# A last projection that takes its PSUM bank when it begins, and a key request half a quad later

## The chip, the cores and the metric

The kernel runs on one core of a Trainium2 chip. The metric is device time in microseconds (us), the median of several executions. TensorE is called PE, VectorE DVE, ScalarE ACT, GpSimd Pool, and SyncE, which issues most DMAs, SP.

## The reference

x is (2, 2048, 512) in fp32. One layer of attention and one linear layer, each with a residual and a layer norm ahead of it:

```
x = x + attention(layernorm(x))      16 heads of 32, 2 groups of keys and values,
                                     rotary tables on q and k, softmax over 2048 keys, then @ wo + bo
x = x + fp8_linear(layernorm(x))     one scale for the whole input, one for the weight,
                                     both rounded to e4m3, product in fp32
```

The one scale of the second part needs the largest magnitude over all tokens, so the second part can begin only when the last token's attention and projection are done.

## The kernel before

**Blocks, quads, units.** The 4096 tokens are eight blocks n of 512 (`TB`), four for each of two batches. The heads are four quads of four. A unit u is half a block (256 queries) of one quad: 64 units, u = 8 n + 2 quad + half. The main loop runs over the units in four rounds r of four key chunks each. Within a round PE makes the shifted scores T (L960), ACT the exponentials p (L969), Pool adds pairs of p (L943) and accumulates them by DMA (L1014, L1016), and PE multiplies p by the values into avs (L910) and sums the pair sums with a matrix of ones (L924). In between, `next(scores)` brings the plain scores of the following unit (PE L517 into s, DVE maximum L524), from which the row maxima come.

**Background work.** Everything else is a generator whose yields name the engine of its next step: `ON_PE`, `ON_DVE` or `OTHER`. A `Job` runs its generator to the first yield when it is made. Jobs stand in three lists, `finishing` (the division of a finished unit, `finish_heads`), `queue` (projections) and `beside` (turning queries, stacking keys, norms). `fill(kind)` takes one step of the first job that is ready and whose next step is of that kind or `OTHER`. The main loop calls `fill(ON_PE)` about seven times in a unit, twice as many in the last two units, and `fill(ON_DVE)` several times.

**The lent bank.** Scores rotate over three PSUM banks s0 to s2. A job that needs PSUM inside the loop calls `bank`, which lends it one of them (`lent[0]`); the scores skip that bank until `give_back`. While a bank is lent, `fill` lets only its owner in `queue` go on, and `do` notes as owner the job whose step made `lent[0]` change. After the loop `attending[0]` is False and the remaining jobs are run to their ends one list after another, in banks of another pool.

**The last block's projection.** For blocks 0 to 6 `finish_block` multiplies the attention by wo (`add_output`, PE L301 into po, DVE L574 adds it to x_res). Block 7 is split: `finish_most` does three of the four chunks of wo for all four token tiles (12 matmuls), and is queued by `finish_heads` of unit 61; `finish_rest` does the fourth chunk for one half (2 matmuls each), queued by `finish_heads` of units 62 and 63. Then come the second norm's statistics, the scale and the fp8 part.

**Keys.** The keys of the attended batch lie stacked in `kS` and `dkS` (two groups, one for quads 0 and 1, one for quads 2 and 3). The next batch's keys are projected during the first batch's blocks, stacked by `stack_keys` and written to DRAM (`halves_far`). `fetch_keys(what, b, g)` issues four DMAs of 256 KB on SP that bring one group into the stack. `stack_next(u)` runs at the start of unit u: on even units it prepares the next quad's queries (calling `advance`, which takes steps of jobs at once, until the query is there) and, in block 3, requests group 0 of batch 1, again calling `advance` until the keys of block 7 are done. Group 1 is requested at the first unit of batch 1.

Of the kernel before, what the change touches and what calls it, by code (L numbers as in the profile page):

```python
# [27 lines left out]
def preln_attn_fp8_ffn_kernel(  # L28
# [38 lines left out]
    B, S, D = x.shape  # L67
    NB = S // TB
# [14 lines left out]
    ON_PE, ON_DVE, OTHER = "PE", "DVE", "other"  # L83
# [268 lines left out]
    def stack(dst, src):  # L352

        for r, part in enumerate(src):
            nc.sync.dma_start(dst(slice(r * HD, (r + 1) * HD)).bitcast(F32), part)

    def fetch_keys(what, b, g):
        far = halves_far[what, b]
        stack(
            lambda rows: stacked[what][rows, g, :],  # L360
            [far[g * HD : (g + 1) * HD, h, :] for h in (0, 0, 1, 1)],
        )
# [76 lines left out]
    keys_done = set()  # L439
# [34 lines left out]
    def stack_queries(k):  # L474

        n, quad = quads[k]
        hi, lo = halves(q_raw.pop((n, quad)), P, f"q_{n}_{quad}")
        qst[k] = wide.tile([P, 4, TB], F32R, tag="qst", name=f"qst_{k}", bufs=2)
        far = dram.tile([P, 2, TB], F32, tag=f"q_far_{k % 2}", name=f"q_far_{k}")
        for h, part in enumerate((hi, lo)):  # L480
            nc.sync.dma_start(far[:, h, :], part.bitcast(F32))
        far = far.rearrange("(j d) h t -> d h j t", j=4)
        read = lambda: stack(
            lambda rows: qst[k][rows, :, :], [far[:, h, :, :] for h in (0, 1, 0, 1)]
        )
        if attending[0]:
            landing.append(read)
        else:
            read()

    def batch(k):
        return quads[k][0] // NB
# [71 lines left out]
    def add_output(n, xt, attn, i, dims=range(DC)):  # L564

        po = bank(f"po_{n}_{i}_{dims[0]}")
        yield from product(
            po,
            lambda c: attn[:, dims[c], i * P : (i + 1) * P],
            lambda c: wo_sb[:, dims[c], :],  # L570
            len(dims),
        )
        yield ON_DVE
        nc.vector.tensor_tensor(xt[:, i, :], po, xt[:, i, :], ALU.add)  # L574
        give_back()

    def second_norm(n, xt, tiles=range(NT)):

        yield from layernorm_stats(
            xt, mean2[:, n, :], rstd2[:, n, :], f"2_{n}_{tiles[0]}", tiles  # L580
        )


        ends = small.tile([P, NT, 2], F32, tag="ends", name=f"ends_{n}_{tiles[0]}")
        for i in tiles:
            for e, op in enumerate((ALU.max, ALU.min)):
                yield ON_DVE
                nc.vector.tensor_reduce(ends[:, i, e : e + 1], xt[:, i, :], AX.X, op)
        at = slice(tiles[0], tiles[-1] + 1)
        yield ON_DVE  # L590
        for e in range(2):
            end = ends[:, at, e]
            nc.gpsimd.tensor_tensor(end, end, mean2[:, n, at], ALU.subtract)
            nc.gpsimd.tensor_tensor(end, end, rstd2[:, n, at], ALU.mult)
        yield LATER
        yield ON_DVE
        nc.vector.tensor_reduce(
            amax2[:, n * NT + tiles[0] : n * NT + tiles[-1] + 1],
            ends[:, at, :],
            AX.X,  # L600
            ALU.max,
            apply_absolute_value=True,
        )
# [15 lines left out]


    def finish_most(n, xt, attn):
        for i in range(NT):
            yield from add_output(n, xt, attn, i, range(DC - 1))

    def finish_rest(n, xt, attn, half):
        tiles = range(half * HT, (half + 1) * HT)
        for i in tiles:
            yield from add_output(n, xt, attn, i, range(DC - 1, DC))
        beside.append(Job(second_norm(n, xt, tiles)))
        y_near[n] = xt  # L630
# [146 lines left out]
    def do(jobs, job):  # L777
        held = lent[0]
        job.step()
        if held is None and lent[0] is not None:  # L780
            owner[0] = job
        if job.kind is None:
            jobs.remove(job)
# [5 lines left out]
    def advance():  # L789
        ready = [job for job in queue if job.due < NEVER and not job.waits()]  # L790
        if lent[0] is not None:
            ready = [owner[0]]
        for jobs, some in ((queue, ready), (beside, list(beside))):
            for job in some[:1]:
                do(jobs, job)
# [21 lines left out]
    def stack_next(u):  # L817
        k, half = units[u]
        n, quad = quads[k]

        if half == 0:
            if k + 1 < len(quads) and k + 1 not in qst:
                while quads[k + 1] not in q_raw:
                    advance()
                stack_queries(k + 1)
            b = batch(k)
            if b + 1 < B and n == (b + 1) * NB - 1:
                if quad == 2:
                    while (b + 2) * NB - 1 not in keys_done:
                        advance()  # L830
                    fetch_keys("kS", b + 1, 0)
                    fetch_keys("dkS", b + 1, 0)
            if b > 0 and n == b * NB and quad == 0:
                fetch_keys("kS", b, 1)
                fetch_keys("dkS", b, 1)

    def ask(u):

# [42 lines left out]
    def finish_heads(u, both, sums):  # L881

        k, half = units[u]
        n, quad = quads[k]
        nc.scalar.copy(both[:, 1, :], sums)  # L885
        for c in range(HB // P):
            yield ON_DVE
            piece = both[:, 1, c * P : (c + 1) * P]
            nc.vector.reciprocal(piece, piece)  # L889
        nc.gpsimd.tensor_tensor(  # L890
            attn_of[n][:, quad, half * HB : (half + 1) * HB], both[:, 0, :], both[:, 1, :], ALU.mult
        )
        if n == NBLK - 1:
            if quad == QUADS - 2 and half == HALVES - 1:
                queue.append(Job(finish_most(n, x_res[n], attn_of[n])))
            elif quad == QUADS - 1:
                queue.append(Job(finish_rest(n, x_res[n], attn_of[n], half)))
        elif quad == QUADS - 1 and half == HALVES - 1:
            job = Job(finish_block(n, attn_of.pop(n)))
            if n not in biased:  # L900
                job.due = NEVER
                without_x[n] = job
            queue.append(job)
# [68 lines left out]
    with tc.manual_schedule():  # L972
        for _ in range(LEAD):
            next(scores)
        for u, (k, half) in enumerate(units):
            n, quad = quads[k]
            if half == 0 and quad == 0:
                attn_of[n] = wide.tile(
                    [P, QUADS, TB], F32, tag="attn", name=f"attn_{n}", bufs=2
                )  # L980
            stack_next(u)
            banks = [
                ps_t.tile([P, 4, HB], F32, tag="EO"[parity], name=f"T_{u}_{parity}")
# [182 lines left out]
```

## Time and profile before

| | us |
|---|---|
| median of 3 runs | 2356.63 (2355.38 to 2365.41) |
| the profiled execution | 2365.06 |
| its span, first to last instruction | 2363.3 |
| PE busy, matmuls | 2145.0 (91%) |
| DVE busy | 1697.7 (72%) |
| Pool busy | 1765.8 (75%) |
| ACT busy | 1231.3 (52%) |
| mean granted TensorE clock | 0.969 |

In the lines of the profile, a group is line, engine, operation, output tile <- input tiles and size, with how often it occurs; in brackets stands how long the engine was idle before it and what released it. "PEld" is PE's weight load, "SPq" a queue's issue of a DMA. In the chain of work that ended last each line is start, duration and what ran. A view of windows has one line per stretch of time: its length, then the busy time and the number of instructions of PE, PEld, DVE, ACT and Pool, the granted clock, the share of DMA engines in use and GB/s.

### The profile page before, as it was taken

To read this page: it belongs to the slowest core of one execution; us is meant where nothing else is said; L and a number is where in the kernel's file an instruction comes from. 1 tells how busy PE (TensorE), PEld (TensorE's weight loads), DVE (VectorE), ACT (ScalarE), POOL (GpSimd) and SP (SyncE) were. 2 spreads that over 40 slices of the span, in tenths; PEclk is the share of its full clock that TensorE was granted. 3 is DMA by queue.
4 is the path that set the end of the run, shared out by engine and by line. 5 is a ranking of instruction groups with operands and counts; after the bars stand their busy time and mean duration, and the time that the engine had idled before them with its cause. 6 is when DMAs were issued, how large, how long until landed. Compare 5 with 4: busy or idle time off the path is not lost. (4 is left out here: it accounts for less than half of the span.)

```text
span 2363.3 us, 39392 instructions
## 1 busy us (share of the span) xinstructions
PE 2145.0 (91%) x15506; PEld 1246.7 (53%) x15506; DVE 1697.7 (72%) x2679; ACT 1231.3 (52%) x1545; POOL 1765.8 (75%) x1199
## 2 busy tenths in 40 slices
PE   5499999999999999999999999999999799899855
PEld 2255555555555555555555555555555455555422
DVE  3467777776687676867767778676876977768378
ACT  2146555655556555645445556454555445555536
POOL 3268889888777987878778878787887777878700
PEclk9689999999999999999999999999999999999977
DMA  6546656666465666657486556564565646847502
GB/s 195 163 102 136 134 117 163 137 138 136 89 167 123 152 134 143 158 116 163 96 204 139 111 118 154 121 120 96 132 146 116 143 91 140 166 85 199 108 32 111
DMA packets 116410, 312.76 MB, mean 132 GB/s; under 512 B 16896, under 2 KB 17536, under 8 KB 112384
## 3 DMA queue, kind: packets, MB, share of 16 engines
q0 software_dynamic: 50160, 175.66, 39.6%
q1 hardware_dynamic: 63648, 133.21, 19.1%
q8 instruction: 121, 1.98, 0.4%
q10 hardware_dynamic: 2416, 1.38, 0.2%
q14 instruction: 65, 0.53, 0.1%
HBM read 91.56 MB, written 42.99 MB: 57 GB/s over the span
## 5 line engine op out<-in xcount | busy, mean ns | idle before, releaser
L524 DVE TENSOR_REDUCE part<-s 128x1 f32<-128x512 f32 x2048 | 1304.8, 683 | 559.6 <-PE s L517 546.0
L943 POOL TENSOR_TENSOR pa<-p,p 128x1024 f32<-128x1024 f32 x511 | 1233.5, 2459 | 300.6 <-ACT p L969 272.7
L969 ACT ACTIVATE p<-T 128x1024 f32<-128x1024 f32 x1024 | 1001.3, 1024 | 590.6 <-PE T L960 564.1
L517 PE MATMUL s<-kS,qst 128*128 128x512 f32 x2048 | 832.4, 465 | 97.0 <-DVE part L524 31.0
L960 PE MATMUL T<-qst,dkS 128*128 128x512 f32 x2048 | 669.7, 423 | 14.4 <-ACT p L969 14.3
L517 PEld LDWEIGHTS s<-kS,qst 128*128 128x128 f32 x2048 | 369.0, 190 | 488.4 <-DVE part L524 256.9
L910 PE MATMUL avs<-p,vX 128*32 128x256 f32 x8192 | 497.7, 383 | 0.8 <-ACT p L969 0.8
L960 PEld LDWEIGHTS T<-qst,dkS 128*128 128x128 f32 x2048 | 365.5, 189 | 161.8 <-ACT p L969 59.4
L910 PEld LDWEIGHTS avs<-p,vX 128*32 128x32 f32 x8192 | 239.7, 110 | 210.4 <-issue 64.7
L1014 POOL DMA_DIRECT2D pa<-pa x255 | 224.3, 880 | 80.4 <-POOL pa L943 75.3
L889 DVE RECIPROCAL both<-both 128x128 f32<-128x128 f32 x128 | 112.4, 919 | 33.8 <-ACT both L885 33.8
L301 PE MATMUL po<-wo_sb,attn 128*128 128x512 f32 x256 | 130.5, 601 | 0.9 <-DVE x_res L574 0.9
L301 PE MATMUL pq<-xnT_q,wq_sb 128*128 128x512 f32 x224 | 113.9, 592 | 0.0
L924 PE MATMUL avs<-pa,ones 128*32 128x256 f32 x1512 | 105.6, 382 | 5.6 <-DMA pa<-pa 5.6
L1032 ACT COPY both<-avs 128x256 f32<-128x256 f32 x64 | 23.8, 373 | 138.3 <-PE avs L910 137.1
L885 ACT COPY both<-avs 128x256 f32<-128x256 f32 x63 | 23.5, 373 | 131.9 <-PE avs L924 131.9
L890 POOL TENSOR_TENSOR attn<-both 128x256 f32<-128x256 f32 x64 | 85.0, 1328 | 6.8 <-DVE both L889 6.8
L951 PEld LDWEIGHTS T<-mT,sel 128*128 128x128 f32 x512 | 80.0, 192 | 12.2 <-issue 0.4
L951 PE MATMUL T<-mT,sel 128*128 128x256 f32 x512 | 82.9, 285 | 0.0
L1016 POOL DMA_DIRECT2D pa<-pa x64 | 74.0, 1156 | 6.5 <-DMA pa<-pa 6.2
L924 PEld LDWEIGHTS avs<-pa,ones 128*32 128x32 f32 x1512 | 49.1, 111 | 39.0 <-DMA pa<-pa 6.5
L503 POOL TENSOR_TENSOR mrow<-mx,mrow 128x8 fp32r<-128x8 f32 x64 | 52.8, 824 | 11.6 <-ACT mrow L532 11.6
(126 smaller groups left out, 1118.7 us busy)
## 6 DMA issues: line engine op xcount, KB each, us to landing
pa<-pa POOLq DMA_DIRECT2D x319, 512.0 KB, 4.7
qst<-q_far SPq DMA_DIRECT2D x128, 256.0 KB, 4.7
x_kv<-in_L_attn_x_dram SPq DMA_DIRECT2D x8, 1024.0 KB, 8.8
q_far<-hi_q SPq DMA_DIRECT2D x32, 256.0 KB, 4.3
q_far<-lo_q SPq DMA_DIRECT2D x32, 256.0 KB, 3.6
x_res<-in_L_attn_x_dram SPq DMA_DIRECT2D x8, 1024.0 KB, 12.3
x_res<-in_L_attn_bo_dram POOLq DMA_DIRECT2D x8, 1024.0 KB, 12.0
out_dram<-v SPq DMA_DIRECT2D x16, 512.0 KB, 2.8
```

Source lines behind the costliest of these rows:

```text
L301: nc.tensor.matmul(dst, lhs(c), rhs(c), start=(c == 0), stop=(c == chunks - 1))
L517: nc.tensor.matmul(s, qst[k][:, j, at : at + P], stacked["kS"][:, group(k), kb * TB : (kb + 1) * TB], start=True, stop=True,)
L524: nc.vector.tensor_reduce(part[:, i, j, kb : kb + 1], s, AX.X, ALU.max)
L889: nc.vector.reciprocal(piece, piece)
L890: nc.gpsimd.tensor_tensor(attn_of[n][:, quad, half * HB : (half + 1) * HB], both[:, 0, :], both[:, 1, :], ALU.mult)
L910: nc.tensor.matmul(av[j * HD : (j + 1) * HD, :], vX[batch(k)][:, kc, group(k), :], p[:, j, :], start=(kc == 0), stop=(kc == NTS - 1), tile ...
L924: nc.tensor.matmul(dst[j * HD : (j + 1) * HD, :], ones, part[:, j, :], start=start and i == 0, stop=stop and i == len(parts) - 1, tile_pos ...
L943: nc.gpsimd.tensor_tensor(pa, a, b, ALU.add)
L951: nc.tensor.matmul(T[:, j, :], sel[:, j, :], maxima[u], start=(j % 2 == 0), stop=True, skip_group_check=True,)
L960: nc.tensor.matmul(T[:, j : j + 2, :], stacked["dkS"][:, group(k), kc * P : (kc + 1) * P], qst[k][:, j : j + 2, half * HB : (half + 1) * H ...
L969: nc.scalar.activation(p, T, AF.Exp, scale=SCALE)
L1014: nc.gpsimd.dma_start(out=far_sums[r], in_=pair, accum_op=ALU.add)
```

## The change

Both generators of block 7's projection begin with `yield OTHER`, as `finish_block` does, so that making the job takes no bank. And the request for group 0 of batch 1's keys, with its `advance` loop, moves from unit 28 (block 3, quad 2, half 0) to unit 29 (half 1). The request for group 1 keeps its place; its condition is written out anew.

```diff
     def finish_most(n, xt, attn):
+        yield OTHER
         for i in range(NT):
             yield from add_output(n, xt, attn, i, range(DC - 1))

     def finish_rest(n, xt, attn, half):
+        yield OTHER
         tiles = range(half * HT, (half + 1) * HT)
...
-            b = batch(k)
-            if b + 1 < B and n == (b + 1) * NB - 1:
-                if quad == 2:
-                    while (b + 2) * NB - 1 not in keys_done:
-                        advance()
-                    fetch_keys("kS", b + 1, 0)
-                    fetch_keys("dkS", b + 1, 0)
-            if b > 0 and n == b * NB and quad == 0:
-                fetch_keys("kS", b, 1)
-                fetch_keys("dkS", b, 1)
+        b = batch(k)
+        if b + 1 < B and n == (b + 1) * NB - 1 and quad == 2 and half == 1:
+            while (b + 2) * NB - 1 not in keys_done:
+                advance()
+            fetch_keys("kS", b + 1, 0)
+            fetch_keys("dkS", b + 1, 0)
+        if b > 0 and n == b * NB and quad == 0 and half == 0:
+            fetch_keys("kS", b, 1)
+            fetch_keys("dkS", b, 1)
```

## The prediction

> **What bounds the kernel now.** The two edits touch two places, so I read those and leave the totals alone. First I cut the span into units, from one copy of a finished unit's sums (ACT L1032) to the next. Unit u is block n = u // 8, quad (u % 8) // 2, half u % 2. The change's first place is units 28 and 29 (block 3, quad 2), the second units 62 and 63 and what follows them. In the view of windows, columns are busy time by engine, granted TensorE clock, DMA share, GB/s. Units 20 to 24 stand first, then 28 to 32.
>
> ```profile
> 773.48:807.75 34.27, 33.63 (x241) 19.44 (x241) 23.25 (x37) 19.02 (x24) 33.01 (x23) 1.00 0.81 190
> 807.75:843.82 36.07, 34.03 (x241) 19.51 (x241) 24.26 (x37) 18.00 (x22) 31.62 (x21) 1.00 0.68 126
> 843.82:877.65 33.83, 33.10 (x239) 19.15 (x239) 24.94 (x38) 17.94 (x23) 29.16 (x20) 1.00 0.61 133
> 877.65:911.87 34.22, 32.80 (x239) 19.22 (x239) 23.35 (x37) 16.85 (x20) 26.82 (x17) 1.00 0.41 78
> 911.87:945.68 33.81, 33.08 (x239) 19.15 (x239) 23.81 (x38) 17.40 (x21) 25.55 (x17) 1.00 0.77 187
> 1038.92:1084.87 45.95, 39.20 (x249) 22.58 (x249) 25.24 (x38) 19.70 (x26) 37.60 (x26) 0.93 0.85 199
> 1084.87:1118.59 33.72, 32.29 (x237) 18.86 (x237) 23.98 (x37) 18.09 (x23) 27.88 (x19) 1.00 0.63 118
> 1118.59:1154.30 35.71, 32.63 (x239) 19.23 (x239) 26.92 (x37) 17.36 (x21) 30.85 (x20) 1.00 0.58 127
> 1154.30:1188.08 33.78, 33.05 (x239) 19.13 (x239) 23.48 (x37) 16.83 (x20) 24.29 (x16) 1.00 0.41 78
> 1188.08:1222.47 34.39, 31.11 (x235) 18.33 (x235) 23.73 (x39) 17.44 (x21) 22.95 (x16) 1.00 0.99 243
> ```
>
> Unit 28 lasts 45.95 us where its neighbours last about 34. The timeline inside it says why.
>
> ```profile
> 1038.73 3.70 PE L301 MATMUL pq<-xnT_q,wq_sb 128*128 128x512 f32 x8
> 1045.92 0.62 ACT L246 CAST hi_kS<-kx 64x512 fp32r<-64x512 f32 x1 [6.11 <-POOL kx L336]
> 1047.18 0.79 PE L517 MATMUL s<-kS,qst 128*128 128x512 f32 x1 [4.52 <-ACT q L450]
> 1076.35 0.70 PE L517 MATMUL s<-kS,qst 128*128 128x512 f32 x2 [1.87 <-DMA qst<-q_far]
> ```
>
> This is the wait loop of `stack_next`: it calls `advance` until the last keys are done, so a whole query projection (8 rows, four instructions) and the key stacking stand in one lump at the head of the unit. ACT waits for Pool's key rotation, the bias copy of the queries stands behind it on ACT, and PE waits 4.52 us for the bank that this copy frees. The clock is at 0.50 from 1047.2 to 1051.2, so a 4-row group takes 1.05 instead of 0.63 us. And qst, queued on SP behind the key loads, holds PE once more at 1076.
>
> The end is read from the chain that ended last (start, duration):
>
> ```profile
> 2233.93 6.59 DMA pa<-pa
> 2240.56 1.93 PE sums_last L924 x16
> 2242.50 14.17 PE po L301 x28
> 2256.69 0.70 DVE x_res L574
> 2257.52 1.97 PE po L301 x4
> 2259.52 0.69 DVE x_res L574
> ```
>
> All 32 projection rows of the last block (one fp32 instruction is two rows) run alone, after the attention. The code says why: `finish_most` takes its bank while the job is being made, inside a `finish_heads` job. `do` then notes that job as the owner of the lent bank, it ends, and `fill` finds no ready job in the queue for the rest of the loop.
>
> **Part 1, keys half a quad later.** The instruction order of the two built programs shows what the scheduler makes of it. In the changed one the lump is gone: the four pq matmuls, the query copy, hi_kS, hi_dkS and Pool's lo_kS, dk, lo_dkS spread over unit 28, and by unit 29 the keys are done, so nothing is forced there. On SP the qst stack, the 1 MB x_res load and sw_q of query 0 now precede the key loads. Units 28 to 32 then carry 7, 7, 2+4, 6 and 6 projection instructions (pq, pq, pq and po, po, po), exactly those of units 20 to 24. So units 20 to 24 price it:
> - before, units 28 to 32: 45.95+33.72+35.71+33.78+34.39 = 183.55;
> - twin, units 20 to 24: 34.27+36.07+33.83+34.22+33.81 = 172.20, that is 11.35 less. The four deferred projections are in it already (unit 32 gets six po for four).
>
> The twin lacks the key loads, eight DMAs of 256 KB each time. Unit 32 has one set, four po and 34.39 us. Unit 25 (no po) lasts 29.25, unit 24 (six) 33.81, so 0.76 per po and 32.29 for four: a set costs up to 2.1 us. Unit 32 keeps its set (+2.1). Unit 29 gets one: 0 at best, as the DMA share there is 0.68; 2.1 at worst by unit 32; I take 1.5, nearer unit 32, because its queue is the same. SP issues them in 3.54+4.00 = 7.5 us (timeline at 1055.5), and in the twin SP has nothing to issue between 805.5 and 814.5, so sw_q of query 1 behind them is hardly late. If that cover were gone, its turn would slip by a round and be taken up at once, since that query is stacked two units on. The keys are read by the next batch's scores from unit 30's last round, some 50 us after the request, against a landing of 6 to 8 us. Sum: -11.35+2.1+1.5 = -7.75. Ends: -11.35 (no load cost) and -5.0 (2.1 in both units and the same again for a late sw_q).
>
> The group-1 request is the same instruction in the same place; it costs nothing.
>
> **Part 2, the bank.** With `yield OTHER` first, `fill` runs the twelve po of `finish_most` inside the loop: 3 in unit 62's last round, 9 in unit 63 (2, 3, 1, 3 by round). Scores are over by then, so the bank is missed by nobody, and `sums_last` takes another one. What is left behind sums_last are four po.
> - Removed at the end: from sums_last's end (2242.43) the last add starts 17.1 us later (2259.52). After: sums copy, two reciprocals and Pool's product end 3.24 after it (2245.67); po_0_3 and po_1_3 (4 rows of 0.43) fit in that; po_2_3 and po_3_3 need the product and take, like the x4 above, 2.03 to the last add. With 0.1 between, 3.24+0.1+2.03 = 5.4. Gain 11.7.
> - Added in units 62 and 63: 24 rows of 0.43 = 10.3 us on PE, and behind each stand the T and avs matmuls that ACT and then Pool wait for. Unit 63 has 23.43-20.11 = 3.3 us of PE idle, unit 62's last round 0.71+0.18+0.43 = 1.3: 5.7 are not covered by gaps. But Pool, not PE, ends the unit: its adds run back to back to 2233, the accumulating DMA lands at 2240.5, and PE's avs were over at 2235.7. Round by round, each po counted at 0.86 less the gap of the timeline that it stands in (0.7 to 0.9 after a round's first T pair, 0.6 before avs), PE falls behind by 1.3 in unit 62's last round, 1.1 in round 0 and 1.25 in round 1; Pool runs 0.5 us behind ACT there, so round 2's adds on Pool, and the DMA after them, come 3.65-0.5 = 3.1 later. I take 3.1; ends 0 and 5.7. A gain is excluded, as nothing on this path is removed.
> - The four adds on DVE (0.69 each): DVE idles 18 us in unit 63, so nothing.
> - `finish_rest` taking its bank later: nothing waits for it before sums_last.
>
> Sum: -11.7+3.1 = -8.6, ends -11.7 and -6.0.
>
> In the window from 2236.0 to 2242.4 PE is mostly idle and gets 0.78, then 0.50 up to 2246.0 and 0.98 after. The Trainium skill ("TensorE: Matmul & The Clock Gate", section "What's actually happening") says that an idle window of about 3.4 us halves the clock and a busy one of that length restores it. This trace agrees (0.50 for 3.6 us). By that rule the fewer PE gaps ahead of sums_last keep the clock full; if it still closed, the estimate would be the second rival's, some 2.6 us later.
>
> **Sum.** 7.75+8.6 = 16.35. The profiled execution took 2365.06 (span 2363.3): it would be 2348.7. It is 8.4 above the median of the runs, 2356.63, and the rows don't say where that lies; both pieces are orders of work that every execution shares, so I subtract the same: 2340.3.
>
> **Rivals.**
> 1. The lump's time comes back. Unit 21, 36.07 us with the heaviest query work, is the one whose twin gets the loads; if they hold up sw_q or Pool's accumulating DMAs there, the 7.75 are lost and 2356.6-8.6 = 2348.0 stays. For: a DMA share of 0.99 in unit 32. Against: that unit is only 2.1 longer. 0.09.
> 2. The clock drops at the end all the same: the last 4 rows at 0.86 instead of 0.43 (+1.7) and half of sums_last's (+0.9): 2342.9. For: Pool and the DMA still end last before sums_last. Against: PE has more to do there. 0.10. This is what the Trainium skill's rule would give if the gap outlived the window.
> 3. PE becomes the bound of unit 63 and all 10.3 us show: tail -11.7+10.3 = -1.4, 2347.5. Against: PE idles 3.3 us there. 0.05.
> 4. Slower: a po that waits for an add or a bank leaves PE idle for some 4 us inside unit 63 and the clock halves there. PE's 20.1+7.7 = 27.8 us would become 55.7 against 23.43: +32.3; with -11.7 and -7.75 that is 2369.4. It decides at a PE gap of 3 to 4 us; the longest now are about 1.1, and the clock is 1.00. 0.04.
>
> That the change doesn't do what it says is excluded by the order of instructions.
>
> **Numbers.** The forecast has 0.72, its own range 2333.6 (both ends on the good side: 23.05) to 2345.6 (5.0+6.0). To hold 8 in 10 the range goes to 2348, over rivals 1 to 3, and to 2332 below, leaving out rival 4 and the scatter of the runs (2355.38 to 2365.41). A measurement tells 0.5% from no change, that is 11.8 us: below 2344.9 lie 0.70 of the forecast's 0.72 and rival 2, so 0.80 faster; 0.02+0.09+0.05 = 0.16 the same; 0.04 slower.
>
> **What would show it.** Right: unit 28 near 34 us with clock 1.00, no PE wait for ACT q at its head; unit 29 at 36 to 38; units 28 to 32 together near 176; the chain's po behind sums_last down from x28 and x4 to eight rows; sums_last ending about 3 us later against unit 62's start. Wrong: unit 29 or 30 above 42 us, a PE wait for kS or qst there, units 62 and 63 together longer by over 6 us, or a clock under 1.00 in unit 63.

## The result and the profile after

The changed kernel took 2344.41 us (median of 4 runs, 2343.33 to 2346.83) against 2359.18 for the kernel before beside it, 14.8 us less: ratio 0.9936, 95% interval 0.9911 to 0.9961. Timed a second time it took 2342.79 against 2363.56: 0.9914 (0.9901 to 0.9928), 20.8 us less. The profiled execution took 2344.18, its span 2342.4, against 2365.06 and 2363.3 before.

The windows of units 28 to 32 after the change, with the columns as before (length; busy time and instructions of PE, PEld, DVE, ACT, Pool; clock, DMA share, GB/s):

```profile
1039.54:1073.85 34.31, 33.67 (x241) 19.44 (x241) 23.24 (x37) 19.03 (x25) 33.05 (x23) 1.00 0.80 190
1073.85:1109.93 36.08, 34.03 (x241) 19.51 (x241) 24.27 (x37) 18.00 (x23) 30.98 (x21) 1.00 0.89 180
1109.93:1143.73 33.80, 33.07 (x239) 19.14 (x239) 25.00 (x38) 17.93 (x22) 29.52 (x20) 1.00 0.64 137
1143.73:1177.97 34.24, 32.78 (x239) 19.22 (x239) 23.35 (x37) 16.86 (x21) 26.85 (x17) 1.00 0.41 77
1177.97:1212.44 34.47, 33.07 (x239) 19.14 (x239) 23.82 (x38) 17.52 (x22) 23.84 (x16) 1.00 0.95 214
```

They last 172.90 instead of 183.55. Against the twin units 20 to 24 the first four differ by 0.04 us at most; the fifth, with the second set of key loads, is 0.66 longer. Unit 28's clock is 1.00 again.

The end, in the chain of work that ended last and in the timeline of PE behind unit 63:

```profile
2225.06 6.56 DMA pa<-pa
2231.66 1.11 PE sums_last L925 x16
2233.27 1.77 DVE both L890 x2
2235.18 0.74 POOL attn L891
2235.96 2.00 PE po L301 x4
2237.98 0.69 DVE x_res L574
```

```profile
2232.66 1.98 PE L301 MATMUL po<-wo_sb,attn 128*128 128x512 f32 x4
2235.96 1.98 PE L301 MATMUL po<-wo_sb,attn 128*128 128x512 f32 x4 [1.31 <-POOL attn L891]
```

Eight po rows are left behind sums_last. The first four run while DVE and Pool make the last quad's product; the other four wait 1.31 us for it. From sums_last's end (2232.77) the last add starts 5.21 later; before it was 17.1. The price stands in units 62 and 63:

```profile
2172.58:2200.89 28.31, 27.62 (x225) 16.52 (x225) 20.61 (x34) 16.76 (x21) 24.22 (x20) 1.00 0.58 126
2200.89:2228.64 27.75, 26.83 (x210) 13.86 (x209) 3.69 (x5) 16.19 (x18) 22.90 (x14) 1.00 0.46 87
```

28.31 and 27.75 for 27.51 and 23.43. I measure the end from unit 61's end to the start of the last add: 74.54 before (2184.98 to 2259.52), 65.40 after (2172.58 to 2237.98), 9.14 less. With 10.65 from units 28 to 32 that is 19.8 of the 20.9 us by which the spans differ. Unit 33 is shorter too, 33.91 for 35.06, so the first place is worth 11.8 in this profile. What is left are units that the change doesn't touch, some longer, some shorter, which cancel here.

### The profile page after: what moved, and what is told of

It reads as the page before. It is cut to its first block, busy times and chain, and to the rows that moved or that the text cites. A ratio compares the mean times of both kernels' runs of the same rounds, so it can differ in the third digit from the quotient of the medians.

```text
span 2342.4 us, 39403 instructions
## 1 busy us (share of the span) xinstructions
PE 2137.7 (91%) x15506; PEld 1243.9 (53%) x15506; DVE 1695.1 (72%) x2679; ACT 1231.1 (53%) x1545; POOL 1765.0 (75%) x1199
## 5 line engine op out<-in xcount | busy, mean ns | idle before, releaser
L952 PEld LDWEIGHTS T<-mT,sel 128*128 128x128 f32 x512 | 79.0, 190 | 12.1 <-issue 0.4
L532 ACT CAST mrow<-mx 128x8 fp32r<-128x8 f32 x64 | 13.1, 205 | 93.4 <-DVE mx L531 93.4
```

Of the source, the lines that this page charges most:

```text
L952: nc.tensor.matmul(T[:, j, :], sel[:, j, :], maxima[u], start=(j % 2 == 0), stop=True, skip_group_check=True,)
```

## The experiments

Units whose code is the same last the same in every kernel to about 0.05 us, apart from a few (8, 32, 40, 41, 48, 52, 53, 58, and 29 by up to 0.5), and unit 0 ends up to 7 us earlier or later. So the medians tell whether, and the units tell where. Unit 33 follows the change: 33.9 us wherever the keys are requested late and nothing is forced in unit 28, 34.5 in e1_bank and e3_lump, 35.06 before; why is not shown.

**e1_bank and e2_keys: each part alone.** e1_bank is the kernel before with

```diff
     def finish_most(n, xt, attn):
+        yield OTHER
...
     def finish_rest(n, xt, attn, half):
+        yield OTHER
```

> Only the two yields; the key request stays in unit 28. If the two parts are independent, this gives the tail alone: units 62 and 63 about 5 us longer together, the stretch from unit 63's end to the last add about 14 us shorter, so 9 us less than the kernel before, unit 28 still at 46. The rival, that the po matmuls cost as much in the loop as they save behind it, gives a change within 2 us.

e2_keys is the changed kernel without these two lines.

> Only the key request half a quad later; the last block's projection as before. Independent parts: units 28 to 32 at 173 instead of 183.5, chain's end with 32 po rows behind sums_last, 8 to 11 us less than the kernel before. The rival, that the lump's time comes back in the following units, gives a change within 2 us.

Measured: e1_bank 0.9972 (0.9961 to 0.9982), 6.9 us less by the medians; e2_keys 0.9951 (0.9936 to 0.9967), 12.3 less. The two together, 19.2, are the change's 20.8 within the intervals: nothing shows that the parts depend on each other. Both rivals (a change within 2 us) fall. e1_bank gained less than the 9 expected, e2_keys more than the 8 to 11; its units 28 to 33 are 12.5 shorter. e1_bank's unit 28 is at 48.62, not at 46: PE waits 3.1 us for qst there instead of 1.9. e1_bank's window of unit 28, then e2_keys' windows of units 28, 29 and 63:

```profile
1033.04:1081.66 48.62, 40.54 (x249) 23.32 (x249) 25.25 (x38) 19.69 (x26) 37.55 (x26) 0.89 0.81 189
```

```profile
1039.80:1074.09 34.29, 33.66 (x241) 19.43 (x241) 23.26 (x37) 19.04 (x24) 33.02 (x23) 1.00 0.83 190
1074.09:1110.16 36.07, 34.02 (x241) 19.51 (x241) 24.27 (x37) 17.98 (x22) 31.68 (x21) 1.00 0.92 181
2199.89:2223.31 23.42, 20.12 (x192) 10.10 (x191) 1.76 (x2) 16.20 (x19) 22.23 (x15) 1.00 0.52 98
```

Each place follows its own part. The end of e1_bank takes 65.46, as in the changed kernel; that of e2_keys 72.52, 2.0 less than the kernel before with the same code there. The difference is in the first po behind sums_last, in e2_keys' chain:

```profile
2229.88 12.24 PE po L301 x28
```

12.24 us for 28 rows is 0.44 a row, at a granted clock of 1.00; before, 14.17 began with 3.6 us at 0.50. So the old end depended on when the clock came back, and the gain at the end is 7 to 9 us.

**e3_lump: the forced steps back in unit 28, the loads at unit 29.**

```diff
+        if b + 1 < B and n == (b + 1) * NB - 1 and quad == 2 and half == 0:
+            while (b + 2) * NB - 1 not in keys_done:
+                advance()
         if b + 1 < B and n == (b + 1) * NB - 1 and quad == 2 and half == 1:
```

> The changed kernel, but unit 28 again forces the jobs on until the last keys are done; the loads stay at unit 29. If the forced lump is the cost, unit 28 is again at 42 to 46 us with a PE wait of some 4 us for ACT q, and the run loses 7 to 10 us of the gain. If the loads queued ahead of qst were the cost, unit 28 is at 34 to 37 and nearly all of the gain stays.

Measured: 0.9961 (0.9947 to 0.9974), 10.1 us less than before: it keeps the gain at the end and little more. Unit 28 lasts 44.19 us, and PE waits at its head as before:

```profile
1042.23 0.50 PE L517 MATMUL s<-kS,qst 128*128 128x512 f32 x1 [4.54 <-ACT q L450]
```

Units 28 to 32 take 180.58, 7.7 more than in the changed kernel. With the loads ahead of qst as well (e1_bank) they take 185.08, 4.5 more again, and PE waits 3.1 us for qst, which e3_lump doesn't. So the lump is the larger part of what was removed, and the loads ahead of qst the smaller (3.0 by the kernel before, 4.5 by e1_bank).

**e4_twice: the eight loads of unit 29 issued twice.**

```diff
             fetch_keys("kS", b + 1, 0)
             fetch_keys("dkS", b + 1, 0)
+            fetch_keys("kS", b + 1, 0)
+            fetch_keys("dkS", b + 1, 0)
```

> The changed kernel with the eight key loads of unit 29 issued twice (the same data again). If a set of loads costs the 2.1 us that the prediction took from unit 32, unit 29 goes from 36.1 to about 38 and the run gets 2 us longer, more if SP's queue of 8 us more delays the turned queries. If the loads are hidden, unit 29 stays at 36.1 and the time within 1 us.

Measured: 0.9951 (0.9935 to 0.9966), 12.1 us less than before where the change gained 20.8. Neither number holds: unit 29 lasts 43.99 us, 7.9 longer. The timelines of DVE and of PE in it say why:

```profile
1106.67 1.85 DVE L319 SCALAR_TENSOR_TENSOR sw_q<-sw_q,sign,cs 128x512 f32<-128x512 f32 x1 [4.65 <-DMA sw_q<-q]
```

```profile
1109.17 1.39 PE L517 MATMUL s<-kS,qst 128*128 128x512 f32 x2 [6.31 <-DVE part L524]
```

SP comes to the swap DMAs of query 1 at 17.5 us into the unit instead of 6.7. The rotation that needs them stands on DVE in front of the score maxima, DVE waits 4.65 us, PE 6.31 for the banks, and the clock is at 0.50 from 1109.2 to 1113.0. This is the first rival's mechanism. One set fits in front of it, two do not.

**e11_more: half a set more** (one more `fetch_keys("kS", b + 1, 0)` in the same place).

> The changed kernel with half a set of key loads more at unit 29 (kS once again, four DMAs, 1 MB). In the changed kernel the rotation of query 1 starts on DVE about 6 us after its swap can have landed, by the 14.7 us from the first swap DMA to the rotation that e4_twice shows. If that slack is what hides the loads, four more DMAs (3.5 to 4 us on SP) still fit and unit 29 stays at 36 to 37. If each load costs in proportion (half of e4_twice's 7.9), unit 29 is at 40.

Measured (one run): unit 29 lasts 37.47, 1.4 longer, between the two expectations. DVE now stands idle for 1.21 us before the rotation:

```profile
1096.89 0.75 DVE L319 SCALAR_TENSOR_TENSOR sw_q<-sw_q,sign,cs 128x512 f32<-128x512 f32 x1 [1.21 <-issue]
```

The swap DMAs start 3.4 us later than in the changed kernel (10.1 into the unit), and the rotation 1.3 us later, so the slack of one set is about 2 us, not the 6 that I read from e4_twice. The profile doesn't name what DVE waited for here; that it is the swap, as in e4_twice, is inferred.

**e9_later: the second set in round 2 of unit 29, behind query 1's swap.**

```diff
+        if n == NB - 1 and quad == 2 and half == 1:
+            fetch_keys("kS", 1, 0)
+            fetch_keys("dkS", 1, 0)
         if half == 0 and quad == 0:
```

> The changed kernel with the second set of key loads of e4_twice, but requested in round 2 of unit 29, behind the swap DMAs of query 1 on SP. If it was the order on SP that made unit 29 last 44.0 us in e4_twice (the swap of query 1 late, DVE waiting for it in order), unit 29 is back at 36 to 38. If the 2 MB of traffic cost it, unit 29 or 30 stays 6 to 8 us longer.

Measured: 0.9915 (0.9901 to 0.9929). Unit 29 is back at 36.92, so it was the order on SP that made it 44 us. The 2 MB are not free all the same: in the profiled execution unit 30 lasts 37.63, 3.8 longer than in the changed kernel. There, by e9_later's timelines of DVE and Pool, the rotation is not late, but long:

```profile
1117.59 4.51 DVE L319 SCALAR_TENSOR_TENSOR sw_q<-sw_q,sign,cs 128x512 f32<-128x512 f32 x1
```

```profile
1116.56 4.99 POOL L947 TENSOR_TENSOR pa<-p,p 128x1024 f32<-128x1024 f32 x2
```

It begins under Pool's two adds and ends 0.55 us after they do. It begins 7.33 us into the unit in both kernels; what moved is Pool, whose adds start 6.30 us into the unit instead of 3.65. Pool's timeline at the end of unit 29 shows what held it up, an issue that waits for an accumulating DMA:

```profile
1105.36 0.85 POOL L1020 DMA_DIRECT2D pa<-pa  x1 [3.63 <-DMA pa<-pa]
```

In the changed kernel Pool doesn't wait there. SP issues the second set from 1090.4 to 1094.5, and the DMA share of that unit is 1.02 instead of 0.89; that this delayed the accumulation is likely, not shown. Two of the five executions took 2340 us, the other three 2346 to 2347 like the profiled one, and the ratio is that of the change: the cost need not come in every execution.

**e5_half and e10_half: half of finish_most in the loop.** The first two token tiles stay in the loop, the others run after it.

```diff
...
-                queue.append(Job(finish_most(n, x_res[n], attn_of[n])))
+                queue.append(Job(finish_most(n, x_res[n], attn_of[n], range(HT))))
+                queue.append(Job(finish_most(n, x_res[n], attn_of[n], range(HT, NT)), due=NEVER))
```

> The changed kernel, but only two of the four token tiles of finish_most go into the loop; the other two (6 po instructions, 12 rows) run after sums_last. If PE is what ends unit 63 and each po there costs most of its 0.86, sums_last ends 1.5 to 3 us earlier, the last add comes 4 to 5 us later after it, and the run is 2 to 3 us longer. If the po were free in the loop, sums_last ends at the same distance and the run is 4 to 5 us longer.

Measured: 0.9931 (0.9919 to 0.9943), 4.4 us longer than the changed kernel. But the edit did another thing too: with half of `finish_most` done early, two po of `finish_rest` came into the loop, and PE met a product that Pool had yet to make:

```profile
2226.21 2.08 PE L301 MATMUL po<-wo_sb,attn 128*128 128x512 f32 x2 [3.98 <-POOL attn L891]
```

Unit 63 lasts 30.81, and those two rows take 2.08 us where two rows elsewhere take 1.02: the granted clock is 0.63 from 2226.2 to 2230.0. It says nothing on the question; it shows the fourth rival in small. e10_half therefore also holds `finish_rest` back (`due=NEVER`).

> Like e5_half, but finish_rest stays behind the loop too, so that PE meets no product of Pool inside unit 63. If PE ends unit 63 and a po costs most of its 0.86 there, the six po that leave the loop bring sums_last 2 to 3 us nearer to unit 61's end (from 60.2 to about 58) and the last add stands about 10 us behind sums_last instead of 5.2: units 62 and 63 and the end together 2 to 3 us longer than in the changed kernel. If po were free in the loop, sums_last stays at 60.2 and the sum is 5 us longer.

Measured (one run), in the windows of units 62 and 63:

```profile
2171.86:2200.18 28.32, 27.62 (x225) 16.50 (x225) 20.61 (x34) 16.77 (x21) 24.24 (x20) 1.00 0.57 126
2200.18:2225.09 24.91, 22.39 (x198) 11.32 (x197) 2.46 (x3) 16.16 (x18) 21.70 (x14) 1.00 0.46 88
```

Unit 63 is 2.84 us shorter for six po fewer, 0.47 each. sums_last ends 58.60 behind unit 61's end instead of 60.19 (1.6 nearer, less than the 2 to 3 expected), the last add starts 9.2 behind sums_last instead of 5.2, and the whole end takes 67.80 instead of 65.40. So a po, 0.86 us on PE, costs about half of that in unit 63's length and 0.27 us at sums_last; behind sums_last it costs 0.67.

**after_again: the change, timed a second time.**

> The changed kernel itself, timed beside the others of this job. From the units of its profile: 20 us less than the kernel before in units 28 to 32 and the end together, of which the medians showed 15. If the parts add up, it stands about 19 us below the kernel before, the sum of what the two parts gave alone (6.9 and 12.3).

Measured: 20.8 us less, given above.

**e8_both: two other lumps taken apart.** On top of the change, block 7's x is loaded later, and the weight's rounding goes to DVE in smaller steps. A third edit, not in the expectation, stands in the same run: in the last unit two of the accumulations by DMA are left out, and sums_last adds their parts by matmul instead.

```diff
-            if n == NBLK - 1:
-                take_x(f"res_{n}")
-                x_res[n] = load_x(n, "res")
-                unbiased.append(n)
+        if n == NBLK - 1 and quad == 2 and half == 0:
+            take_x(f"res_{n}")
+            x_res[n] = load_x(n, "res")
+            unbiased.append(n)
...
             magic = t2(f"w_magic_{o}")
+            yield ON_DVE
             yield from round_e4m3(w[o], v, magic)
...
         nc.vector.tensor_tensor(v, v, magic, ALU.add)
+        yield ON_DVE
         nc.vector.tensor_tensor(dst, v, magic, ALU.subtract)
...
                 if not (last and whole):
                     far_sums.append(add_pair(u, chunks[2], *probs[2:]))
-                    nc.gpsimd.dma_start(out=far_sums[r], in_=pair, accum_op=ALU.add)
-                if r == 2:
+                    if whole and r == 2:
+                        loose = [pair]
+                    else:
+                        nc.gpsimd.dma_start(out=far_sums[r], in_=pair, accum_op=ALU.add)
+                if r == 2 and not whole:
                     nc.gpsimd.dma_start(out=far_sums[1], in_=far_sums[0], accum_op=ALU.add)
...
-        sum_up(sums, [pair, *probs[2:], *far_sums[1:]], True, True)
+        sum_up(sums, [*far_sums, *loose, pair, *probs[2:]], True, True)
```

> The changed kernel with two other lumps taken apart in the same spirit: block 7's x is loaded in unit 60 instead of beside block 6's in unit 56 (unit 58 lasts 40.7 us, with a DMA wait of 4.3 us on PE), and the FFN weight's rounding goes to DVE in single steps (unit 52 lasts 40.4 us, with a PE wait of 5.0 us for DVE). If these waits are the price, units 52, 53 and 58 fall to about 35, 34 and 36 and the run gets some 8 us shorter, less 2 to 4 us for the steps that now stand in units 56 and 57. If the work merely moves, the time stays within 2 us.

Measured: 2329.24 us, 0.9855 (0.9841 to 0.9868) of the kernel before, 13.6 less than the changed kernel timed beside it. Its windows of units 52, 53, 57 and 58:

```profile
1834.41:1867.44 33.03, 29.47 (x234) 17.41 (x234) 32.23 (x46) 18.30 (x22) 29.59 (x20) 1.00 0.76 156
1867.44:1902.74 35.30, 32.76 (x239) 19.23 (x239) 27.46 (x40) 16.91 (x21) 28.07 (x18) 1.00 0.43 82
2001.41:2032.44 31.03, 28.45 (x231) 16.97 (x231) 29.04 (x47) 17.66 (x21) 25.51 (x20) 1.00 0.56 103
2032.44:2066.57 34.13, 32.33 (x239) 19.27 (x239) 26.50 (x43) 17.35 (x22) 27.89 (x18) 1.00 0.65 139
```

They were 40.75, 37.13, 29.77 and 40.43 in after_again's profile. Unit 56, which takes part of the weight's steps, goes from 28.62 to 32.65, unit 57 from 29.77 to 31.03; units 52 to 58 together are 12.6 shorter, more than the 4 to 6 expected, and unit 61 is 1.0 longer. PE's waits of 5.0 us for DVE and of 4.3 us for a DMA, which the changed kernel has in this stretch, are gone. The place of the third edit is 0.8 us shorter: from unit 61's end to the start of the last add it is 64.58 us, for 65.40 in the changed kernel. The three edits were not run apart. This is the fastest kernel of the study.

## Why the prediction was right

The direction, both mechanisms and their places hold, and 2344.4 lies in the range. The step to an absolute time was helped by chance: by the units and by the second timing the gain is nearer to 20 than to the 16.35 predicted (14.8 by the first), while the kernel before ran at 2359 to 2364 here, above the 2356.63 that I subtracted from.

- **The twin units** were the best step: 34.27, 36.07, 33.83, 34.22 predicted units 28 to 31 within 0.04 us each, deferred projections included.
- **The load term was mis-sized.** I put 1.5 us on unit 29 and 2.1 on unit 32; they cost 0.0 and 0.7 in the profile after (0.5 and 0.6 in after_again), and unit 32 lasts 33.79 in e2_keys, no more than its twin. Most of the 3.5 us by which the sum fell short lie here. The 2.1 was a real wait, but not the price of a set. PE's waits in unit 32 (us in total, times, longest), before and then after:

```profile
PE mtp L543 <- POOL mrow L503: 2.1, 1, 2.1
```

```profile
PE mtp L543 <- POOL mrow L503: 0.8, 1, 0.8
```

  In e2_keys this wait is missing, with the same loads requested in the same place. The step for mrow stands on Pool behind an issue that waits for an accumulating DMA, by Pool's timeline before:

```profile
1218.43 0.85 POOL L1016 DMA_DIRECT2D pa<-pa  x1 [3.28 <-DMA pa<-pa]
```

  After the change Pool waits 2.72 us there, in e2_keys 1.83. So PE pays for an accumulation that lands too late for it, and one unit's 2.1 was no price for the next. What made it land earlier is not shown. The slope of 0.76 us per po is not what failed: without these waits (2.1 and 0.6 for qst before, 0.8 after) unit 32 is about 31.7 with four po and 33.7 with six.
- **Unit 33 is not in the sum at all.** It is 1.15 us shorter, in e2_keys as in the changed kernel.
- **The cover was right, what lies behind it wrong.** I wrote that a late sw_q would slip by a round and be taken up at once. e4_twice shows 7.9 us instead: the rotation's place on DVE is fixed when the program is built, so DVE waits in it. The first rival did not happen, but it stands only about 2 us away (e11_more), and its other condition, Pool's accumulating DMAs held up, is what PE felt in unit 32 and Pool in e9_later.
- **The end**: 11.7 predicted behind sums_last, 11.9 measured (17.1 to 5.2). About 2 us of that are luck of the clock: in e2_keys the same old end takes 15.1, which leaves 9.9. 3.1 late at sums_last predicted, 2.7 measured at its end (60.19 for 57.45 from unit 61's end); its last 16 rows begin 3.5 later, and are 0.8 shorter at the full clock. e10_half confirms that PE ends unit 63 in part, which the walk by rounds gave.
- **The second rival** did not come: the clock was 1.00 from 2231.6 to 2236.0, and sums_last's last 16 rows took 1.11 instead of 1.93. The first of PE's two gaps ahead of it had shrunk, by PE's timelines before and then after; the second is 0.79 for 0.78:

```profile
2238.23 0.64 PE L924 MATMUL sums_last<-pa,ones 128*32 128x256 f32 x8 [2.51 <-POOL pa L943]
```

```profile
2229.37 0.64 PE L925 MATMUL sums_last<-pa,ones 128*32 128x256 f32 x8 [0.85 <-POOL pa L944]
```

  The Trainium skill ("TensorE: Matmul & The Clock Gate", section "What's actually happening"), as weighed in the prediction, has the clock halved by an idle window of about 3.4 us. The trace after agrees: no such window, no halved clock. The trace before shows that less was enough: no gap there was longer than 2.51 us, PE was busy for 3.40 of the 6.40 us from 2236.0 to 2242.4, and the clock was at 0.50 behind them. Here the measurement decides.
- **The third** is refuted by e1_bank: not all 10.3 us show, but 2.7 at sums_last. **The fourth** did not happen in the changed kernel; e5_half shows that a gap of 3.98 us in unit 63 is enough for it to begin.

## What to carry to other kernels

Where units of work repeat, find the unit that already does what the change would bring, and price the change with it whole. A wait that one execution shows beside a transfer is not the price of that transfer elsewhere: ask which engine's step was late, and behind what. A forced loop in a builder ("go on until X is done") looks like nothing in the code and was a lump here on PE and ACT at once: look for units that last longer than their neighbours, and ask half a unit later. Before a transfer is put ahead of others on one queue, find whose operands come behind it and how many us they have to spare.

## What the runs showed of the hardware

The same 128x512 rotation on DVE (two operands in SBUF) took 0.65 us where Pool had just finished its adds and 4.51 where it began under them, as shown in e9_later. In the changed kernel's unit 30 it took 1.86, and in after_again's unit 29, the one that is 0.5 us longer, 1.20. In these three it ended 0.55 to 0.57 us after Pool's adds did. The Trainium skill ("SBUF — State Buffer", section "SBUF: two separate sides") says that such an instruction and a Pool one that reads SBUF lock each other out of a shared port for a whole instruction. These rows agree, except that DVE in e9_later sat through two of Pool's adds.
